# One GpSimd power of eight columns for two lengths in the block's residual sums

## The chip, the cores and the metric

The kernel runs on one core of a Trainium2 chip. The time is the device time of one execution in microseconds, as the median of several runs. The profile is one further execution, recorded by the hardware profiler; its times count from the first instruction of the span.

## What is computed

The reference is a stack of four stages over `x` (8 batches of 512 tokens, 256 features, float32): a mixture of experts, a segmented memory attention, a hyperbolic transformer block with adaptive layer norm, and two layers of windowed attention with a gated feed-forward. The change lies in the third stage, at its two residual sums:

```python
_norm = lambda x: sqrt(sum(x * x)).clip(EPS)          # EPS = 1e-7
logmap0 = lambda x: arctanh(clip(_norm(x), EPS, 1 - 1e-5)) * x / _norm(x)
expmap0 = lambda v: tanh(_norm(v)) * v / _norm(v)
def mobius_add(x, y):
    x2, y2, xy = sum(x * x), sum(y * y), sum(x * y)
    num = (1 + 2 * xy + y2) * x + (1 - x2) * y
    return num / (1 + 2 * xy + x2 * y2).clip(EPS)
...
attn_t = g_msa * logmap0(attn_out)
x = mobius_add(residual, expmap0(attn_t))
...
ff_t = g_mlp * logmap0(ff)
return mobius_add(residual, expmap0(ff_t))
```

Both sums take a projection `u`, which stands for a point of the ball by its tangent (`attn_out = expmap0(u)`). So `logmap0` of it is `u` times a factor `f` of at most 1 that holds its length under `MAX_LEN`, the arctanh of the clip. The tangent is then `gate * u * f`, its length `n`, and `y = tanh(n) / n` times it.

## The kernel before, in words

All 8 batches of 512 tokens lie in SBUF as `X`, tokens on the 128 partitions, in `NT` = 4 tiles of tokens a batch. A number per token is therefore a tile of 128 x 4. The instruction streams of the five engines are written out by hand: generators yield once a beat, and `Beats.advance` lets every live generator take one step a beat, the urgent ones first and the bulk ones last. What is issued earlier in this order stands earlier in the in-order queue of its engine.

`last_stages` runs the block. Its main loop has 32 steps a batch, in which `attention` issues scores (`s`), exponentials (`pt`, L1209) and values (`oT`). Beside it run, each as a generator: `block.begins` (layer norm and q, k, v of a later batch, with the evictions at L985 and sums at L975), `middle(b)` (squares of the heads' outputs, lengths, the scaling of `o` at L1250, one half on VectorE and one on GpSimd, its transposition `flip`, the output projection `wo`, and the first residual sum), and `end(b)` (layer norm, the scaling of `v` at L1289, the feed-forward with `f1` and `f2`, and the second residual sum). `end(b)` is started when a `middle` has finished and the step in the batch is `END_AT` = 4; in the last batch it is started as soon as a `middle` has finished. After the last attention step the drain follows: a loop (L1390 to L1399) in which the remaining `middle` and `end` run, and in every second beat one step of the windowed layers (`layers.beat`, up to `LAYERS_FIRST`). When nothing of the block is left, `until_end.close()` frees its memory, `open_rest` issues the layers' weight loads on the SP queue, and the layers go on with a step a beat. Their shifted rows `h<-X` (L1724, L1726) use the same SP queue.

A residual sum has two parts. `sums` takes the projection tile by tile: ScalarE squares `u` with an accumulated sum (`u2`, L1066), GpSimd multiplies by the gate (L1099), and VectorE forms the sums of (gate u)^2 (`a2`) and gate u x (`xa`) (L1069). `joined` makes the two factors per token from these and applies them: ScalarE scales `X` by `e` (L1147), VectorE adds `cb` times the gated tangent (L1142), in a loop of five beats.

Lengths come from `Norms`. `inverse` clamps a squared length at `EPS * EPS` (VectorE, L860), and raises it to the power -0.5: for at most `NT` columns by one GpSimd operation (L862), for wider ones by the eight VectorE operations of `rsqrt_steps` (L817 to L826). It yields a beat behind the power. `length` multiplies clamp and power to the length (L872). `shorten` turns the power into the factor f (L879).

`joined` now makes two such powers, one behind the other: `shorten(u2)` gives f; f squared times `a2` (L1119, L1120) is the squared length of the tangent, and `length` of that gives n and 1/n. Then ScalarE takes tanh(n) (L1122). The squared length of y is s * s * a2 (L1127, L1128). It yields a beat behind each power, one before the step of L1126, one before L1133 and one before the loop.

Of the kernel before, what the change touches and what calls it, by code (L numbers as in the profile page):

```python
# [14 lines left out]
ALU = mybir.AluOpType  # L15
# [5 lines left out]
NT = SEQ // P  # L21
# [35 lines left out]
EPS = 1e-7  # L57
MAX_TANH = float(np.float32(1.0 - 1e-5))

MAX_LEN = math.atanh(MAX_TANH)  # L60
# [749 lines left out]
def rsqrt_steps(nc, x, y, t):  # L810

    bits = lambda a: a.bitcast(mybir.dt.int32)
    mul, stt = nc.vector.tensor_mul, nc.vector.scalar_tensor_tensor
    nc.vector.tensor_scalar(bits(y), bits(x), -0.5, float(0x5F3759DF), ALU.mult, ALU.add)  # L817
    mul(t, x, y)
    mul(t, t, y)
    stt(t, t, -10.0 / 3, t, ALU.add, ALU.mult)  # L820
    yield
    stt(y, t, 5.0, y, ALU.add, ALU.mult)
    yield
    mul(t, x, y)
    stt(t, t, -27.0 / 1024, y, ALU.mult, ALU.mult)
    stt(y, t, 9.0 / 16, y, ALU.add, ALU.mult)  # L826
# [18 lines left out]
class Norms:  # L845
# [10 lines left out]
    def inverse(self, n2, tag):  # L856

        nc, w = self.k.nc, n2.shape[1]
        c, r = self.new(w, f"{tag}c"), self.new(w, f"{tag}r")
        nc.vector.tensor_scalar_max(c, n2, EPS * EPS)  # L860
        if w <= NT:
            nc.gpsimd.tensor_tensor(r, c, self.k.mhalf.to_broadcast([P, w]), ALU.pow)  # L862
            yield
        else:
            yield from rsqrt_steps(nc, c, r, self.new(w, f"{tag}t"))
        return c, r
# [149 lines left out]
def last_stages(k, A, out, block):  # L1016


    nc, tc = k.nc, k.tc
    D = DIM  # L1020
    nq = CH // 4
    bank, acc = block.bank, block.bank.acc
    bank.all = False
    S, Q, begun = block.S, block.Q, block.begun
    with ExitStack() as stack:
# [31 lines left out]
        def adaptive(b, lo, n, tag):  # L1057
            out = p.tile([P, n, D], F32, tag=tag, name=tag)
            nc.sync.dma_start(
                out=out.rearrange("p n d -> p (n d)"),  # L1060
                in_=k.ada[b : b + 1, lo * D : (lo + n) * D].to_broadcast([P, n * D]),
            )
            return out
# [9 lines left out]
        def flip(src, out):  # L1073

            for kc in range(2):
                tp = bank("flip")
                for t in range(NT):
                    k.tr(tp[:, t * P : (t + 1) * P], src[:, t, kc * P : (kc + 1) * P])
                yield URGENT
                nc.vector.tensor_copy(out[:, kc, :], tp)  # L1080
# [32 lines left out]
        def joined(nm, xs, x2, u, acc):  # L1113

            u2, a2, xa = acc
            mul, stt = nc.vector.tensor_mul, nc.vector.scalar_tensor_tensor
            f = yield from nm.shorten(u2)
            n3, s, e, cb = (nm.new(NT, f"j_{i}") for i in ("n3", "s", "e", "cb"))
            mul(n3, f, f)  # L1119
            mul(n3, n3, a2)  # L1120
            n, r = yield from nm.length(n3, "j_l")
            nc.scalar.activation(s, n, AF.Tanh)  # L1122
            mul(f, r, f)
            nc.vector.tensor_scalar(cb, x2, -1.0, 1.0, ALU.mult, ALU.add)
            yield
            mul(s, s, f)  # L1126
            mul(n3, s, s)  # L1127
            mul(n3, n3, a2)  # L1128
            stt(e, xa, 2.0, s, ALU.mult, ALU.mult)
            mul(cb, cb, s)  # L1130
            mul(s, x2, n3)
            yield
            stt(s, s, 1.0, e, ALU.add, ALU.add)  # L1133
            nc.vector.tensor_scalar_max(s, s, EPS)
            nc.vector.reciprocal(s, s)
            stt(e, e, 1.0, n3, ALU.add, ALU.add)
            mul(cb, cb, s)
            mul(e, e, s)
            yield
            for t in range(NT + 1):  # L1140
                if t:
                    nc.vector.scalar_tensor_tensor(  # L1142
                        xs[t - 1], u[:, t - 1, :], cb[:, t - 1 : t], xs[t - 1],
                        ALU.mult, ALU.add,
                    )
                if t < NT:
                    nc.scalar.activation(xs[t], xs[t], AF.Copy, scale=e[:, t : t + 1])  # L1147
                yield

        def tiles(b):  # L1150
            return [k.X[:, b * NT + t, :] for t in range(NT)]
# [68 lines left out]
        def middle(b):  # L1220

            middles.append(b)
            nm, o, x2, xs = norms["m"], S[b]["o"], S[b]["x2"], tiles(b)
            gate = adaptive(b, 2, 1, "ada_m")[:, 0, :]
            h2 = nm.new(NT * CH, "oh2")
            for t in range(NT + 1):
                if t:
                    nc.vector.reduce_sum(
                        h2[:, (t - 1) * CH : t * CH],
                        sq.rearrange("p (h d) -> p h d", d=CHD),  # L1230
                        AX.X,
                    )
                if t < NT:
                    sq = p.tile([P, D], F32, tag="sqm", name="sqm")
                    nc.scalar.activation(sq, o[:, t, :], AF.Square)
                yield
            w = yield from nm.shorten(h2, 1.0 / BETA_RATIO)
            nc.vector.tensor_mul(h2, h2, w)
            nc.vector.tensor_mul(h2, h2, w)
            o2 = nm.new(NT, "o2")  # L1240
            nc.vector.reduce_sum(o2, h2.rearrange("p (t h) -> p t h", h=CH), AX.X)
            f = yield from nm.shorten(o2)
            w3 = w.rearrange("p (t h) -> p t h", h=CH)
            nc.vector.tensor_mul(w3, w3, f.unsqueeze(2).to_broadcast([P, NT, CH]))
            for i in range(2):
                ts = slice(2 * i, 2 * i + 2)
                o3 = o[:, ts, :].rearrange("p t (h d) -> p (t h) d", d=CHD)
                w2c = w[:, 2 * i * CH : 2 * (i + 1) * CH]
                eng = nc.gpsimd if i else nc.vector
                eng.tensor_mul(o3, o3, w2c.unsqueeze(2).to_broadcast([P, 2 * CH, CHD]))  # L1250
            yield
            yield
            oT = k.area(3).rearrange("p (c n) -> p c n", c=2)
            yield from flip(o, oT)
            acc = [nm.new(NT, f"j_{i}") for i in ("u2", "a2", "xa")]
            pps = {}

            def project():
                for t in range(NT):
                    pps[t] = bank("wo")[:, :D]  # L1260
                    for kc in range(2):
                        k.mm(pps[t], oT[:, kc, t * P : (t + 1) * P], wo[:, kc, :], kc == 0, kc == 1)
                    yield

            def evict(t, out):
                nc.vector.tensor_add(out, pps[t], b_o)

            pr = project()
            next(pr)
            yield  # L1270
            for _ in sums(xs, o, gate, acc, evict, lambda t: t in pps):
                next(pr, None)
                yield
            if b == NB - 1:
                layers.open_wo()
            yield from joined(nm, xs, x2, o, acc)
            waiting.append(b)

        def end(b):

            nm, xs = norms[f"e{b % 2}"], tiles(b)
            rows = adaptive(b, 3, 2, "ada_e")
            v = p.tile([P, NT, D], F32, tag="v_e", name="v", bufs=2)
            v2, x2 = yield from modulated(
                nm, xs, rows[:, 0, :], rows[:, 1, :], v, block.junk[0]
            )
            f = yield from nm.shorten(v2)
# [5 lines left out]
            uT = p.tile([P, NFC, SEQ], F32, tag="uT", name="uT")  # L1293
            sq = p.tile([P, SEQ], F32, tag="sqs", name="sqs")
            pps, sqs, f2, made, summed = {}, {}, {}, [], []
            acc = [nm.new(NT, f"j_{i}") for i in ("u2", "a2", "xa")]

            def f1():
                for fc in range(NFC + 1):
# [51 lines left out]
            f = yield from nm.shorten(n2)  # L1351
# [6 lines left out]
            for _ in sums(xs, v, gate, acc, evict, lambda t: t in f2):  # L1358
                next(pr, None)
                yield  # L1360
            yield from joined(nm, xs, x2, v, acc)

        n = 8 * nq
# [4 lines left out]
        for i in range(8 - HEADS_AHEAD, NB * n + 2):  # L1370
            if i >= 0:
                next(steps, None)
            b, r = divmod(i + BEGIN_AHEAD, n)
            if r == 0 and b < NB:
                start(block.begins(b))
            if (i + HEADS_AHEAD) % 8 == 0 and 0 <= i + HEADS_AHEAD < NB * n:
                start(block.heads((i + HEADS_AHEAD) // 8))
            if waiting and (i % n == END_AT or i > (NB - 1) * n):
                start(end(waiting.pop(0)))
            beats.advance()  # L1380
            if len(begun) == NB:
                begun.clear()
                layers.open_weights()
# [5 lines left out]
        i, even = PROJECT_AT - 8 * TILES_AHEAD, True  # L1389
# [625 lines left out]
```

## Time and profile before

| what | us |
|---|---|
| median of 3 runs (3374.48 to 3377.88) | 3377.74 |
| the profiled execution | 3374.69 |
| its span, first to last instruction | 3372.9 |
| first and last start of L1122, the Tanh of joined | 1299.1 and 2047.0 |
| GpSimd's power in joined, L862 to `j_lr` (16, mean) | 1.084 |

The mean clock granted to TensorE is 0.974 of full speed. Reading: the page gives busy time by engine, and the span in 40 slices with the busy share in tenths. A row of a view by line names engine, operation, output <- input by the program's names, shapes and count. The chain of waits is the sequence of work that ended last, each piece released by the one before it. In a timeline, a row's own duration may overlap the next one's on its engine. VectorE's busy time in the stretch from 1890 to 1900 us is 8.69 us of 10, TensorE's 4.59, and from 1980 to 1990 us 7.04 and 3.82. The largest waits of TensorE in the span are

```profile
PE q L83 <- DVE hT L1529: 24.1, 10, 8.1
PE flip L87 <- DVE o L1250: 17.4, 8, 7.6
PE prT L87 <- POOL pr L1664: 12.0, 7, 3.9
PE s L83 <- ACT pt L1209: 7.3, 3, 3.5
PE flip L87 <- ACT v L1289: 6.9, 1, 6.9
```

with the total, the count and the longest of each in us.

### The profile page before, as it was taken

Reading aid. Unit: us, or ns where it says so; the run is one execution under the profiler, and the core shown is the slowest. Engines: PE = TensorE matmul, PEld = TensorE weight load, DVE = VectorE, ACT = ScalarE, POOL = GpSimd, SP = SyncE. Lnnn points to the kernel's source line nnn. Section 1 sums busy time; section 2 is a strip of 40 time slices with the busy share of each in tenths; the row PEclk is TensorE's granted clock in tenths of the full one; section 3 lists DMA queues with packets and bytes.
Section 4 is the critical chain, followed back from the end, with each engine's and each line's share of the span. In section 5 each row is a group of like instructions: output and inputs, shape, how many; then the busy total and the mean of one; then the engine's idle time right before and its main releaser. Section 6 shows DMA issues by size and latency. Waiting matters only on the chain.

```text
span 3372.9 us, 45689 instructions
## 1 busy us (share of the span) xinstructions
PE 3238.6 (96%) x16359; PEld 1875.6 (56%) x16359; DVE 1943.6 (58%) x6003; ACT 1714.9 (51%) x3626; POOL 968.2 (29%) x932
## 2 busy tenths in 40 slices
PE   9999999999999999999999777999999999999998
PEld 4444444456666643544444445666666666666665
DVE  3211111145657847778875667776666767777773
ACT  3112121244454477666666434666666666666663
POOL 2000000032322212333333333333333334433332
PEclk9999999999999999999999889999999999999999
DMA  5111111000000010000010001000000000000000
GB/s 195 59 42 53 56 59 58 0 9 14 8 17 19 21 46 11 10 6 10 10 35 7 12 2 64 4 4 4 4 4 5 4 21 25 17 18 17 17 16 28
DMA packets 37075, 85.30 MB, mean 25 GB/s; under 512 B 4931, under 2 KB 29504, under 8 KB 33776
## 3 DMA queue, kind: packets, MB, share of 16 engines
q0 software_dynamic: 5152, 42.52, 3.6%
q1 hardware_dynamic: 26960, 33.56, 3.1%
q10 hardware_dynamic: 4736, 6.29, 0.6%
q8 instruction: 130, 2.13, 0.3%
q14 instruction: 97, 0.79, 0.1%
HBM read 69.73 MB, written 8.44 MB: 23 GB/s over the span
## 4 chain that ended last, share of the span: by engine, by line
PE 62%; DVE 10%; ACT 4%; POOL 1%; issue 1%; DMA 0%; SPq 0%; ACTq 0%; POOLq 0%; DVEq 0%
PE f L83 6%; PE w L83 4%; PE o L83 4%; PE g L83 4%; PE wo L83 4%; PE a L83 4%; PE sc L83 3%; PE prT L87 3%; PE v L83 3%; PE s L83 3%; PE q L83 3%; PE k L83 3%; PE proj L83 3%; PE oT L83 3%; PE qkv L83 2%; PE qkTp L87 2%
## 5 line engine op out<-in xcount | busy, mean ns | idle before, releaser
L1664 POOL TENSOR_TENSOR pr<-pr,sums 128x1024 f32<-128x1024 f32 (+1 forms) x128 | 215.1, 1681 | 672.0 <-DVE sums L1663 650.4
L1652 ACT ACTIVATE pr<-pr,nmx,rn 128x256 f32<-128x256 f32 (+1 forms) x512 | 287.4, 563 | 177.4 <-DVE nmx L1637 177.0
L391 DVE TENSOR_TENSOR hT<-hT,wm 128x512 f32<-128x512 f32 x128 | 88.9, 695 | 474.8 <-ACT hT L387 364.3
L1209 ACT ACTIVATE pt<-s 128x512 f32<-128x512 f32 x512 | 264.3, 611 | 140.6 <-PE s L83 140.5
L387 ACT ACTIVATE hT<-ph,wR 128x512 f32<-128x512 f32 x128 | 87.9, 687 | 351.1 <-PE ph L83 351.1
L83 PE MATMUL ph<-ccT,wR 128*128 128x512 f32 x512 | 240.6, 592 | 0.0
L83 PE MATMUL py<-hT,wR 128*128 128x512 f32 x512 | 240.5, 592 | 0.0
L83 PE MATMUL s<-qkT,qkT 16*128 16x512 f32 x1024 | 185.3, 666 | 9.6 <-ACT pt L1209 7.3
L83 PE MATMUL w<-w2w,g 128*128 128x256 f32 x768 | 187.6, 383 | 0.0
L1630 DVE CUSTOM_DVE_ANT_0 pr<-sc,wB 128x256 f32<-128x256 f32 (+1 forms) x512 | 168.2, 383 | 0.3 <-PE sc L83 0.3
L83 PEld LDWEIGHTS w<-w2w,g 128*128 128x128 f32 x768 | 141.3, 190 | 46.2 <-issue 32.3
L87 PE MATMUL prT<-ident,pr 128*128 128x128 f32 x1152 | 154.2, 275 | 12.3 <-POOL pr L1664 12.0
L198 POOL DMA_INDIRECT wR<-in_w_e_dram,erow x16 | 15.7, 982 | 523.0 <-PE py L83 261.4
L83 PEld LDWEIGHTS py<-hT,wR 128*128 128x128 f32 x512 | 97.1, 190 | 123.2 <-issue 123.2
L83 PEld LDWEIGHTS ph<-ccT,wR 128*128 128x128 f32 x512 | 97.3, 190 | 122.5 <-issue 122.5
L83 PE MATMUL g<-hnT,w 128*128 128x512 f32 x320 | 153.6, 603 | 0.5 <-DVE hnT L1772 0.5
L87 PEld LDWEIGHTS prT<-ident,pr 128*128 128x128 f32 x1152 | 132.9, 143 | 37.3 <-POOL pr L1664 17.2
L83 PE MATMUL oT<-pt,v_aug 128*32 128x512 f32 x1024 | 146.1, 634 | 6.2 <-ACT oS L1174 4.7
L83 PE MATMUL a<-hnT,w 128*128 128x512 f32 x320 | 150.4, 592 | 0.0
L387 ACT ACTIVATE hT<-ph,wS 128x512 f32<-128x512 f32 x64 | 44.0, 687 | 175.3 <-PE ph L83 172.5
L83 PE MATMUL ph<-ccT,wS 128*128 128x512 f32 x256 | 124.2, 608 | 2.8 <-DMA wS<-in_w_s_dram 2.0
L1779 DVE SCALAR_TENSOR_TENSOR g<-a,cols,gl 128x512 f32<-128x512 f32 x80 | 59.9, 748 | 114.8 <-PE a L83 96.8
(410 smaller groups left out, 7201.0 us busy)
## 6 DMA issues: line engine op xcount, KB each, us to landing
x1d<-X SPq DMA_DIRECT2D x32, 128.0 KB
x<-x1d POOLq DMA_DIRECT2D x32, 128.0 KB, 2.4
h<-X SPq DMA_DIRECT2D x64, 63.5 KB
w<-in_w_d_dram SPq DMA_DIRECT2D x2, 1386.0 KB
X<-in_x_dram SPq DMA_DIRECT2D x4, 512.0 KB
wB<-in_w_b_dram SPq DMA_DIRECT2D x1, 2048.0 KB
ada_e<-ada SPq DMA_DIRECT2D x8, 256.0 KB
out_dram<-X ACTq DMA_DIRECT2D x16, 128.0 KB
```

The lines of the kernel that those rows point to most:

```text
L83: self.nc.tensor.matmul(out, lhsT=lhsT, rhs=rhs, start=start, stop=stop)
L87: self.nc.tensor.transpose(out, in_, self.ident[:n, :n])
L198: nc.gpsimd.indirect_dma_start(out=w, out_offset=None, in_=A["w_e"], in_offset=bass.IndirectOffsetOnAxis(ap=erow[:, b, j : j + 1], axis=0),)
L387: nc.scalar.activation(hT, ph, AF.Gelu_apprx_tanh, bias=w[:, 4 * HID + fc : 4 * HID + fc + 1])
L391: nc.vector.tensor_mul(hT, hT, wm[b][:, j, :])
L1209: nc.scalar.activation(pts[-1][:, h % 2, :], ss[h], AF.Exp, scale=1.0 / math.sqrt(CHD))
L1630: nc.vector.tensor_tensor_reduce(prs[-1][:, a, i % 2, :], s[:, a, :], win, 1.0, LEAST, ALU.add, ALU.max, nmx[:, pair, i % 2 : i % 2 + 1],)
L1652: nc.scalar.activation(pr[:, a, h, :], pr[:, a, h, :], AF.Exp, bias=nmx[:, 2 * half + a, h : h + 1], scale=rn[:, i : i + 1], accum_out=sum ...
L1664: nc.gpsimd.tensor_mul(prs[half], prs[half], s.unsqueeze(3).to_broadcast([P, 2, 2, nw * P]))
L1779: nc.vector.scalar_tensor_tensor(g[r, c, :], pa, cols(4 + c, r), gl[r], ALU.add, ALU.mult)
```

## The change

`u2` and `a2` become the two halves of one tile of eight columns, `nm.pairs`, and one clamp and one GpSimd power of eight columns give 1/|u| and 1/|gate u|. The limit of width up to which `inverse` uses GpSimd is raised to eight columns; no other caller has a width between five and eight. From the two: f = min(MAX_LEN / |u|, 1), n = a2 / |gate u| * f, clamped at EPS, and f / n by VectorE's reciprocal. y's squared length is tanh(n) squared. One of the yields goes with the second power, so all behind it in `joined` is issued a beat earlier than it was.

```diff
@@ Norms.inverse
         nc.vector.tensor_scalar_max(c, n2, EPS * EPS)
-        if w <= NT:
+        if w <= 2 * NT:
             nc.gpsimd.tensor_tensor(r, c, self.k.mhalf.to_broadcast([P, w]), ALU.pow)
             yield
@@ joined
             u2, a2, xa = acc
             mul, stt = nc.vector.tensor_mul, nc.vector.scalar_tensor_tensor
-            f = yield from nm.shorten(u2)
-            n3, s, e, cb = (nm.new(NT, f"j_{i}") for i in ("n3", "s", "e", "cb"))
-            mul(n3, f, f)
-            mul(n3, n3, a2)
-            n, r = yield from nm.length(n3, "j_l")
+            s, e, cb, f, n, y2 = (nm.new(NT, f"j_{i}") for i in ("s", "e", "cb", "f", "n", "y2"))
+
+            _, r = yield from nm.inverse(nm.pairs, "j_l")
+            nc.vector.tensor_scalar(f, r[:, :NT], MAX_LEN, 1.0, ALU.mult, ALU.min)
+            mul(n, a2, r[:, NT:])
+            mul(n, n, f)
+            nc.vector.tensor_scalar_max(n, n, EPS)
             nc.scalar.activation(s, n, AF.Tanh)
-            mul(f, r, f)
+            nc.vector.reciprocal(n, n)
+            mul(f, n, f)
             nc.vector.tensor_scalar(cb, x2, -1.0, 1.0, ALU.mult, ALU.add)
             yield
+            mul(y2, s, s)
             mul(s, s, f)
-            mul(n3, s, s)
-            mul(n3, n3, a2)
             stt(e, xa, 2.0, s, ALU.mult, ALU.mult)
             mul(cb, cb, s)
-            mul(s, x2, n3)
+            mul(s, x2, y2)
             yield
             stt(s, s, 1.0, e, ALU.add, ALU.add)
             nc.vector.tensor_scalar_max(s, s, EPS)
             nc.vector.reciprocal(s, s)
-            stt(e, e, 1.0, n3, ALU.add, ALU.add)
+            stt(e, e, 1.0, y2, ALU.add, ALU.add)
@@ middle and end, each
-            acc = [nm.new(NT, f"j_{i}") for i in ("u2", "a2", "xa")]
+            nm.pairs = nm.new(2 * NT, "j_ua")
+            acc = nm.pairs[:, :NT], nm.pairs[:, NT:], nm.new(NT, "j_xa")
```

## The prediction

> **What bounds the kernel now.** I read the page first, then the busy time by stretches, then the chain of waits inside two stretches, then single rows.
>
> ```profile
> PE 3238.6 (96%) x16359; PEld 1875.6 (56%) x16359; DVE 1943.6 (58%) x6003; ACT 1714.9 (51%) x3626; POOL 968.2 (29%) x932
> ...
> PE   9999999999999999999999777999999999999998
> ```
> TensorE is busy 96% of 3372.9 us; only three slices, some 1855 to 2110 us, fall to 7 tenths. The edited functions run only between 1290 and 2060 us. The view by stretches (window, length, then busy us of PE, PEld, DVE, ACT, POOL, and the clock) splits that:
>
> ```profile
> 1400.00:1500.00 100.00, 97.06 (x487) 49.06 (x486) 75.62 (x255) 65.31 (x147) 34.70 (x37) 0.93 0.04 9
> ...
> 1900.00:1950.00 50.00, 37.07 (x117) 21.15 (x116) 41.03 (x124) 18.35 (x46) 22.14 (x20) 0.84 0.05 16
> 1950.00:2000.00 50.00, 32.07 (x104) 19.38 (x103) 32.82 (x124) 17.99 (x54) 15.80 (x16) 0.70 0.01 3
> ```
> One batch of Block takes about 99 us (flips of `o` at 1343.4 and 1442.1) with TensorE at 97%. The drain, where the last batch has no attention left beside it, leaves TensorE 31 of 100 us idle and its clock down to 0.70. A change of this size can win something in two places: the drain, and any part of a batch where "busy" matmuls follow another engine. The chain of waits from 1410 to 1445 us shows such a part (start, length, what):
>
> ```profile
> 1438.54 0.02 issue
> 1438.56 0.18 DVE shc L860
> 1438.74 0.07 issue
> 1438.81 1.18 POOL shr L862
> 1439.99 0.02 issue
> 1440.02 0.18 DVE shr L879
> ...
> 1440.59 1.51 POOL o L1250
> 1442.10 0.04 issue
> 1442.14 1.54 PE flip L87 x6
> ```
> From 1416.3 to 1438.7 us every piece of it is VectorE; it ends in GpSimd's half of L1250, and TensorE's flips wait for that. The sums of `end` (joined) lie inside this VectorE run. The sums of `middle` do not: around 1473 to 1498 us the chain is TensorE nearly throughout.
>
> **VectorE's part.** Each of the 16 joined calls has 20 small VectorE operations now and 19 after (one fewer each). Their pieces on the chain of the batch above: 0.08 (L860) + 0.66 (L879, L1119, L1120, L860) + 0.24 (L872, L1123, L1124) + 0.79 (L1126 to L1131) + 0.75 (L1133 to L1138) = 2.52 us. A piece that reads its predecessor's output costs some 0.19 us with its issue gap, one that doesn't some 0.07. The new order: 0.08 + (0.09 + 0.07 + 0.19 + 0.19 + 0.20 + 0.19 + 0.08 = 1.01) + (0.08 + 0.07 + 0.19 + 0.07 + 0.09 = 0.50) + 0.75 = 2.34 us. That is 0.18 us less for each call that lies on the path; beside TensorE-bound work it is nothing.
>
> **What moves.** joined gives way once less, so all behind its first power is issued one beat (a round of the interleaved generators) earlier. In the order of the built program TensorE's own sequence is unchanged until the drain, because `end` starts at a fixed step of each 32. What does move in front of something: in five batches one `X<-v` update (L1142) now stands ahead of VectorE's half of L1250. In the chain above VectorE is just done with L975 when the power returns (1439.98 against 1439.99), so this update is fully exposed: 0.39 us (its increment on the chain at 1910.67 to 1913.8 is 0.40). ScalarE's Tanh moves too, in `middle`, ahead of four exponentials that it used to follow: it must wait for the fourth VectorE operation behind the power, some 0.85 us after ScalarE would have reached the exponentials (1477.45). The matmuls that read these start at 1483.70 and the last exponential ended at 1479.51, so 4.2 us cover it: nothing; without that cover it would be 7 x 0.85 = 6 us. No DMA is moved against another on its queue.
> Batches: 5 x (0.39 - 0.18) = +1.0 us.
>
> **The power of eight columns.** No row has one. The nearest is the same operation on four:
>
> ```profile
> L862 POOL TENSOR_TENSOR j_lr<-j_lc,mhalf x16: 1006/1012/1922, 1297.8 to 2045.4; 128x4 f32<-128x4 f32 x16
> ```
> (min/median/max in ns.) Low end: 1.01 us, if nothing depends on the width. High end without contention: GpSimd's multiplies of 256 and 512 columns take 753 and 1333 ns (L1099, L1317), so 173 ns are fixed, and 0.84 us of the power belongs to its four columns; doubled, 1.85 us. The Trainium skill (GPSIMD Engine Reference, section 3.1, Elementwise) gives some 2.6 cycles an element at 1.2 GHz for two inputs, an estimate of 9 ns for four more columns, so 1.02 us. But by that price the four-column power itself would be near the fixed cost and not six times it, so I take the row: 1.85 us. It replaces two powers of 1.01, of which only the first was ever waited for.
>
> Does the wider power hold VectorE up? The Trainium skill (SBUF — State Buffer, "SBUF: two separate sides") speaks against the change: VectorE and GpSimd take a shared pair of ports as an exclusive lock for a whole instruction, so that a VectorE operation with two SBUF inputs waits until GpSimd's ends. By it each power would block VectorE, for up to 1.85 us in place of 1.01, in the five exposed stretches some +4 us. The timeline says it for the adds of squares and not for the power (start, length):
>
> ```profile
> 1478.01 0.15 DVE L903 TENSOR_TENSOR log<-log,log 128x4 f32<-128x4 f32 x1
> ...
> 1478.42 0.16 DVE L905 TENSOR_TENSOR log<-log,log 128x4 f32<-128x4 f32 x1
> ...
> 1483.25 1.13 DVE L1127 TENSOR_TENSOR j_n<-j_s 128x4 f32<-128x4 f32 x1
> ```
> L905 runs at its usual 0.16 us within the power of 1478.18 to 1479.22; L1127 takes 1.13 us under an add of squares (1480.24 to 1485.71). So the port costs 0 here, with +4 us as the other end.
>
> Waits for its result: in the exposed stretch VectorE is busy with other work from 1423.87 (end of L860) to 1426.81 (L879), 2.9 us, so 1.85 us stay hidden. In the drain the cover is thinner.
>
> **The drain.** Counting the beats that the loops issue, it falls from 76 to 74, and ends at step 19 of the windowed layers, not 20: one such step (2.6 us each: 1313 us of the rest by some 500 steps) goes behind it. By its joined calls:
> - `end(5)`, 1888 to 1914 us: VectorE is the chain, but for the Ln table, the Tanh table and the Tanh on ScalarE (1896.4 to 1899.9), for which VectorE idles 0.73 us. The new order has that Tanh before the Ln table, where Exp's table serves. -0.73 - 0.18, and +0.5 because only 1.4 us of other VectorE work follow L860 before the result is read: -0.4.
> - `middle(7)`, 1932 to 1948: GpSimd loses a slot of 1.01 and one of 1.92 us and gets 1.85 ahead of the adds of squares; VectorE waits 0.47 us now, some 1.3 then. Its four-column operations swell to 0.8 to 1.2 us under the adds, in a pattern the order changes. I take 0, from -2 to +1.
> - `end(6)`, 1974 to 1994: only 0.55 us cover the power, +0.9 over today's 0.50 wait. TensorE waits 6.88 us for the flips of `v`, whose scaling (L1289) today stands behind a second set of exponentials on ScalarE (1988.98 to 1990.89); the new order puts it ahead: -1.9. Together -1.0.
> - `end(7)`, 2039 to 2078: the power is covered by 1.3 us (L1576), +0.4; -0.18. After it, L1731 waits 2.50 us for the shifted rows `h<-X`, which queue behind the layers' weights; the weights now get one step more of lead, so TensorE's 1.42 us behind that go. Together -1.2.
> Drain: -0.4 + 0 - 1.0 - 1.2 = -2.6 us.
>
> **Sum.** +1.0 - 2.6 = -1.6 us on the profiled execution: 3374.69 to 3373.1 (its span 3372.9, with 1.8 us around it). That execution lies 3.05 us under the median of the runs; on the median, 3377.74 - 1.6 = 3376.1 us. The range of this case alone is 3370 to 3383.
>
> **Rivals.**
> 1. The drain pays fully, and the power doesn't grow with its width. For it: 245 us by 76 beats is 3.2 us a beat; two fewer, less the step moved behind, is -3.8; the flips (-1.9) and the rows (-1.4) make it -7.1; a flat power takes off the added waits (0.5 + 0.8 + 0.9 + 0.4 = 2.6), +1.0 stays from the batches: -8.7, of which I leave some 1.5 for what is counted twice, since a shorter beat is partly the same flips. 3377.74 - 7.2 = 3370.5. Against it: the stretches are VectorE-bound, and VectorE keeps its work.
> 2. Slower: the eight-column power is slow where it meets VectorE's traffic. A row speaks for it: one four-column power took 1.92 us, which doubled is 3.8. It decides from 2.9 us, where the cover of the batches ends: 5 x 1.0 = +5 us there, and in the drain 4 x 1.95 = +7.8: 3376.1 + 12.8 = 3389. Against it: 1.92 is the largest of 16, the median 1.01.
> 3. It does nothing that can be measured because everything is hidden: 3377.7. This falls in the first case.
>
> **Chances.** About 0.2% (6.8 us) is what a measurement of this kernel can tell from no change. The sum above and the third rival: 0.67, within it. The first rival 0.18, faster. The second 0.15, slower. The range goes a little into both: 3369 to 3386.
>
> **What would show it.** Right: L862 with eight columns near 1.85 us, 16 GpSimd and 16 VectorE instructions fewer, flips of `o` 99 us apart, TensorE idle between 1880 and 2080 us less by 2 to 3 us. Wrong: the period of a batch moves by over 0.5 us; VectorE waits for L862 in a batch; ScalarE's exponentials appear as what TensorE waits for after 1475; the stall at the flips of `v` stays at 7 us. The weakest terms are the width's price, and the order in the drain, where a shift by one beat realigns every queue.

## The result, and the profile after

The changed kernel takes 3405.58 us in the median (3403.45 to 3408.84, 4 runs) against 3376.86 us before (3374.48 to 3377.88, 4 runs). The ratio is 1.0089, with a 95% interval of 1.0077 to 1.0101: slower by some 29 us. The profiled execution has a span of 3402.9 us, 30.0 more than before. The forecast was 3376.1 us, no change, with a range of 3369 to 3386.

The page of the changed kernel, its busy time:

```profile
PE 3255.0 (96%) x16359; PEld 1874.3 (55%) x16359; DVE 1945.4 (57%) x5987; ACT 1714.4 (50%) x3626; POOL 958.8 (28%) x916
```

VectorE and GpSimd have 16 instructions fewer each, as the change says; VectorE is busy for 1.8 us more all the same, GpSimd for 9.4 us less. TensorE, with the same 16359 matmuls, is busy for 16.4 us more. So part of the loss does not show as idle time: the rows of the same matmuls are longer, because they run at a lower rate or because a wait is hidden in them. The view by stretches, from the flips of `o` of the second batch to those of the sixth (window, length, then busy us of PE, PEld, DVE, ACT, POOL, and the clock), first before, then after:

```profile
1342.50:1738.00 395.50, 382.42 (x1920) 191.04 (x1920) 298.59 (x1005) 260.05 (x582) 136.74 (x145) 0.94 0.03 8
```
```profile
1341.60:1758.50 416.90, 395.18 (x1921) 188.09 (x1921) 297.77 (x998) 259.30 (x583) 131.68 (x137) 0.92 0.03 8
```

Four batches take 21.4 us more. TensorE's idle time in them grows from 13.1 to 21.7 us, and its busy time by 12.8 us for the same work. Each of them takes 102.3 to 105.9 us, where it took 98.8 to 99.0. The rest of the 30 us: 0.8 us are won before, 2.3 us in the next batch, 5.2 us are lost up to the last flips of `o` (1909.5 and 1932.9) and 6.6 us behind them. Over two thirds of the loss lie in the batches, where I had counted +1.0 us.

What TensorE waits for in those four batches (engine and line that waits, what it waits for, us in total, times, longest), before and after. The windows, 1340 to 1740 and 1340 to 1760, take in the flips of the second batch as well:

```profile
PE flip L87 <- DVE o L1250: 9.0, 5, 2.1
PE oT L83 <- ACT oS L1174: 2.6, 4, 0.7
PE flip L87 <- POOL o L1250: 1.4, 5, 0.5
PE s L83 <- DVE ccT L985: 1.1, 1, 1.1
```
```profile
PE s L83 <- DVE ccT L985: 8.2, 4, 2.0
PE s L83 <- DVE uT L1307: 6.5, 4, 1.6
PE oT L83 <- ACT oS L1176: 3.0, 4, 0.8
PE flip L87 <- ACT v L1292: 2.4, 3, 0.8
PE flip L87 <- DVE o L1252: 0.7, 1, 0.7
```

The wait that I had costed, for L1250 (L1252 now), is gone from the four batches: the 0.7 us left are those of the second batch's own flips. Two others have come: the scores `s` wait for VectorE's evictions `uT` (L1303 before, L1307 now) and `ccT` (L985). They don't read `uT`: the code's seven PSUM banks rotate among all users, and the last two of a group of eight `s` get a bank that this eviction has yet to empty. The timeline of VectorE ahead of that wait (start, length), before and after, and GpSimd's adds of squares beside it in the changed kernel:

```profile
1380.22 0.74 DVE L1303 TENSOR_SCALAR uT<-f,cols 128x512 f32<-128x512 f32 x1
...
1381.10 1.89 DVE L940 SCALAR_TENSOR_TENSOR ccT<-X,mv,wB 128x256 f32<-128x256 f32 x2
1382.91 0.74 DVE L1303 TENSOR_SCALAR uT<-f,cols 128x512 f32<-128x512 f32 x1
```

```profile
1379.67 0.74 DVE L1307 TENSOR_SCALAR uT<-f,cols 128x512 f32<-128x512 f32 x1
1380.33 0.15 DVE L1129 TENSOR_TENSOR j_y<-j_s 128x4 f32<-128x4 f32 x1
...
1380.98 1.14 DVE L1133 TENSOR_TENSOR j_s<-x,j_y 128x4 f32<-128x4 f32 x1
1382.04 1.88 DVE L940 SCALAR_TENSOR_TENSOR ccT<-X,mv,wB 128x256 f32<-128x256 f32 x2
1383.84 0.74 DVE L1307 TENSOR_SCALAR uT<-f,cols 128x512 f32<-128x512 f32 x1
```
```profile
1380.83 5.57 POOL L1321 TENSOR_TENSOR sqs<-sqs,sq 128x512 f32<-128x512 f32 x4
```

Between the last two `uT` there now stand the five small operations L1129 to L1133 of `middle`'s joined. They take 1.71 us together, since the fifth falls under GpSimd's adds of squares and takes 1.14 us. Before, three such operations stood there (L872, L1123, L1124) for 0.22 us, and the six operations that the five replace (L1126 to L1131) followed the `uT`, at 1384.19 to 1386.97. From one `uT` to the next it was 2.69 us and is 4.17. What TensorE does behind it, before and after:

```profile
1382.71 2.11 PE L83 MATMUL s<-qkT,qkT 16*128 16x512 f32 x8
1384.76 1.07 PE L83 MATMUL oT<-pt,v_aug 128*32 128x512 f32 x8
1385.76 3.72 PE L83 MATMUL f<-wC,uT 128*128 128x256 f32 x16
1389.40 1.14 PE L83 MATMUL s<-qkT,qkT 16*128 16x512 f32 x8
```
```profile
1381.88 1.13 PE L83 MATMUL s<-qkT,qkT 16*128 16x512 f32 x6
1384.63 1.88 PE L83 MATMUL s<-qkT,qkT 16*128 16x512 f32 x2 [1.62 <-DVE uT L1307]
1386.44 1.94 PE L83 MATMUL oT<-pt,v_aug 128*32 128x512 f32 x8
1388.31 5.38 PE L83 MATMUL f<-wC,uT 128*128 128x256 f32 x16
1393.61 1.14 PE L83 MATMUL s<-qkT,qkT 16*128 16x512 f32 x8
```

The changed kernel is 0.83 us ahead at 1381.9 and 4.21 us behind at 1393.6: 5.04 us are lost. From the start of `s` to that of `oT` it is 2.51 us more, of which 1.62 is the stall; the other 2.53 are matmuls at a lower rate: eight `oT` take 1.94 us and not 1.07, sixteen `f` 5.38 and not 3.72. The granted clock (third number from the end of the row) of 1384.6 to 1393.6 is 0.62; at the same place before it is 1.00. After, then before:

```profile
1384.60:1393.60 9.00, 8.96 (x26) 4.68 (x26) 5.70 (x15) 4.34 (x12) 2.99 (x3) 0.62 0.00 0
```
```profile
1383.76:1392.76 9.00, 9.00 (x55) 5.09 (x53) 7.24 (x22) 7.16 (x18) 4.39 (x4) 1.00 0.01 2
```

The place ahead of L985 is the same story: VectorE's timeline has the five operations again (`end`'s joined, 1435.10 to 1436.50), and one thing more:

```profile
1432.35 0.18 DVE L1125 RECIPROCAL j_n<-j_n 128x4 f32<-128x4 f32 x1 [0.70 <-ACT j_s L1124]
```
L1125 waits 0.70 us for ScalarE's Tanh. It writes its reciprocal over `n`, which the Tanh still reads. Over the kernel VectorE waits 6.9 us in 16 waits for that; the prediction has no such term.

### The profile page after: what moved, and what is told of

The parts are those of the page before. It is cut to its first block, busy times and chain, and to the rows that moved or that the text cites. A ratio compares the mean times of both kernels' runs of the same rounds, so it can differ in the third digit from the quotient of the medians.

```text
span 3402.9 us, 45648 instructions
## 1 busy us (share of the span) xinstructions
PE 3255.0 (96%) x16359; PEld 1874.3 (55%) x16359; DVE 1945.4 (57%) x5987; ACT 1714.4 (50%) x3626; POOL 958.8 (28%) x916
## 4 chain that ended last, share of the span: by engine, by line
PE 59%; DVE 12%; ACT 4%; issue 2%; POOL 2%; DMA 0%; ACTq 0%; POOLq 0%; DVEq 0%
PE f L83 5%; PE o L83 4%; PE w L83 4%; PE g L83 4%; PE a L83 4%; PE wo L83 4%; PE sc L83 3%; PE prT L87 3%; PE q L83 3%; PE v L83 3%; PE k L83 3%; PE proj L83 3%; PE s L83 3%; PE oT L83 2%; PE qkv L83 2%
## 5 line engine op out<-in xcount | busy, mean ns | idle before, releaser
L83 PE MATMUL oT<-pt,v_aug 128*32 128x512 f32 x1024 | 153.7, 665 | 6.2 <-ACT oS L1176 5.7
L83 PE MATMUL f<-wC,uT 128*128 128x256 f32 x512 | 126.6, 400 | 1.3 <-DVE uT L1307 1.3
```

The lines of the kernel that those rows point to most:

```text
L83: self.nc.tensor.matmul(out, lhsT=lhsT, rhs=rhs, start=start, stop=stop)
```

## The experiments

Theory of order: with a beat fewer, the five operations stand ahead of evictions that TensorE waits for. Rivals: the wide power, the wait for Tanh, the shorter drain, another PSUM bank for `s`, and, for the size of the loss, the slow matmuls. Ratios are to the kernel before, which had a median of 3374.31, 3375.76 and 3374.81 us beside experiments 1 to 4, 5 to 8 and 9 to 11.

**1. An empty beat behind the power, in both callers.**
```
 _, r = yield from nm.inverse(nm.pairs, "j_l")
+yield
```


> The changed kernel with one more empty beat behind the eight-column power in joined, so that everything behind it stands in the beat where it stood in the kernel before; power, arithmetic and instruction counts stay as changed. Order theory (five small operations of the sums, L1129 to L1133, and the wait for Tanh at L1125 now stand ahead of the evictions that TensorE waits for): the loss of some 29 us goes nearly all, 3375 to 3382 us, and TensorE no longer waits 1.6 us for uT near 1384. Power theory (the eight-column power, or its 1.63 us on GpSimd, holds VectorE up): the loss stays, 3400 or more.

3382.69 us, ratio 1.0021 (1.0014 to 1.0028), 0.7 us above the expected range. The wide power and the whole arithmetic are still there, and 23 of 30 us are gone, by the ratios; the wait for `uT` is gone too. The wide power is not the cause. But in this program the last two `s` of the group also have a bank that no `uT` empties (weight loads of `s` wait for `uT` in 4 places, 8 in the changed kernel), and so it is in experiments 2 and 11; what the order alone does is seen in 5 and 6. Four batches take 394.8 us (before 395.5); what is left lies behind: 83.9 us up to the last flips of `o` against 78.8.

**2. The empty beat in `middle` only.**
```
+if nm.name == "m":
+    yield
```


> The empty beat in the sums of middle only; the sums of end stay one beat early. Order theory: the stalls at uT (about +5.0 us a batch, between 1375 and 1396) go, those at the eviction of qkv before the flips of o (about +1.7 a batch) stay: some 4 x 5 = 20 of 29 us are won back, 3382 to 3388. If both places were one stall that only moves, 3400.

3378.81 us, ratio 1.0013 (1.0004 to 1.0022), better than expected; within the intervals it can't be told from the beat in both callers. Its waits in the four batches:

```profile
PE s L83 <- DVE ccT L985: 8.2, 4, 2.0
PE oT L83 <- ACT oS L1178: 3.0, 4, 0.8
PE flip L87 <- ACT v L1294: 1.7, 2, 0.8
```
The waits for `uT` are gone, those for L985 are as in the changed kernel, and yet four batches take 399.5 us. The wait ahead of the flips is thus worth some 4 us of its 8.2, for it takes the place of the old one at the flips.

**3. The empty beat in `end` only** (the same with `!= "m"`).

> The empty beat in the sums of end only; the sums of middle stay one beat early. Order theory: the stall at uT and what follows it stay, +5.0 us in each of four or five batches, while the place before the flips of o goes back: 3393 to 3400. If the sums of end were the cause (the stretch that the prediction took for the bound one): 3380.

3397.92 us, ratio 1.0065 (1.0048 to 1.0082). The waits of `s` for L985 shrink to 2.3 us in four, those for `uT` stay at 6.5 in four, and most of the loss with them. `end`'s sums, where I had looked for the risk, are the minor place.

**4. The reciprocal in another tile.**
```
-nc.vector.reciprocal(n, n)
-mul(f, n, f)
+nc.vector.reciprocal(y2, n)
+mul(f, y2, f)
```


> The changed kernel, its reciprocal written to another tile, so that VectorE need not wait until ScalarE's Tanh has read n (0.70 us at L1125 in the batch of 1432, 0.27 us near 1378). Order theory: the five operations still stand ahead of uT, so most of the loss stays; 0.7 us less ahead of the eviction of qkv: 3394 to 3403. If that wait is the cause of the stalls: 3380.

3398.17 us, ratio 1.0067 (1.0050 to 1.0084): some 7 us of the loss by the ratios (its interval and that of the changed kernel overlap, from 1.0077 to 1.0084), with the stall at `uT` down from 1.62 to 1.39 us. At most a contribution, not the cause.

**5. Only the five operations a beat later, in both callers; beats, power, Tanh and drain as changed.**
```
+yield
 mul(y2, s, s)
 ...
 mul(s, x2, y2)
-yield
 stt(s, s, 1.0, e, ALU.add, ALU.add)
```


> The changed kernel with the same number of beats, in which only the five operations L1129 to L1133 are issued one beat later, with the six that follow them; power, Tanh, the X updates and the fall of the drain by two beats stay as changed. Order theory: the five operations no longer stand ahead of uT, the stall of 1.62 us at s goes in each batch, and most of the 24 us that the empty beat in middle won come back by this alone: 3378 to 3388. Rival (the earlier Tanh, the earlier X updates or the shorter drain make the loss): it stays at 3400 to 3406.

3381.29 us, ratio 1.0016 (1.0008 to 1.0023). This is the narrowest of the repairs, and it wins 25 of 30 us. VectorE at the same place:

```profile
1379.21 0.74 DVE L1307 TENSOR_SCALAR uT<-f,cols 128x512 f32<-128x512 f32 x1
1379.87 0.87 DVE L940 SCALAR_TENSOR_TENSOR ccT<-X,mv,wB 128x256 f32<-128x256 f32 x2
1380.66 0.74 DVE L1307 TENSOR_SCALAR uT<-f,cols 128x512 f32<-128x512 f32 x1
```
The last `uT` follows 1.45 us behind the one before it. L940, which took 1.88 us under GpSimd's adds, now comes for the most part ahead of them (they start at 1380.37) and takes 0.87. Four batches take 395.5 us, as before the change. `s` has the same waits for VectorE in this built program as in the changed kernel (8 weight loads of it wait for `uT`, for 3.7 us and not 12.8), so it is the order and no other bank that removes the stall.

**6. The empty beat in `middle`, and the reciprocal in another tile** (2 and 4 together).

> The empty beat in the sums of middle only, together with the reciprocal written to another tile. Order theory: the two repairs add up where the wait for Tanh still stands ahead of an eviction (0.70 us before L985 in end): stall of 2.04 us at s before the flips of o shrinks, 3373 to 3377, the time of the kernel before or a little less. If the wait for Tanh only mattered together with the stall at uT: 3378 to 3380, as with the empty beat alone.

3386.35 us, ratio 1.0036 (1.0022 to 1.0049): a miss. Taking a wait away made it some 8 us slower than experiment 2, by the ratios, though 18 of 30 us are still won. VectorE's order is the same, but a score group has another bank in this built program, one that `uT` empties:

```profile
1381.78 1.13 PE L83 MATMUL s<-qkT,qkT 16*128 16x512 f32 x6
1383.42 1.12 PE L83 MATMUL s<-qkT,qkT 16*128 16x512 f32 x2 [0.51 <-DVE uT L1309]
1384.47 1.69 PE L83 MATMUL oT<-pt,v_aug 128*32 128x512 f32 x8
1386.09 4.74 PE L83 MATMUL f<-wC,uT 128*128 128x256 f32 x16
```
Even this stall of 0.51 us is followed by slow matmuls (4.74 us for sixteen `f`), in all four batches, which take 408.5 us (2: 399.5). That the bank alone makes the difference is read from the trace; no run isolates it.

**7. The empty beat in `middle` always and in `end` for the first six batches, and the reciprocal in another tile.**
```
-yield from joined(nm, xs, x2, v, acc)
+yield from joined(nm, xs, x2, v, acc, b < NB - 2)    # True in middle: an empty beat
```


> The empty beat in middle for all batches and in end for the first six, not for the last two, whose sums lie in the drain; reciprocal to another tile. With the empty beat everywhere the batches took 486.9 us from the second to the seventh flip of o (488.3 before) but the stretch after it 83.9 (78.8 before). If both readings hold and add up: 3370 to 3375, faster than before. If the loss after the seventh flip comes from the empty beat in middle: 3376 to 3382.

3386.44 us, ratio 1.0032 (1.0020 to 1.0043): a miss, with the same wait for `uT` as in 6 (2.0 us in four).

**8. Six memsets ahead of the last `uT`, on top of 6.**
```
+if i == NFC - 1:
+    for _ in range(6):
+        nc.vector.memset(idle, 0.0)
 nc.vector.tensor_scalar(uT[:, i, :], ...)
```


> The kernel with the empty beat in middle and no wait for Tanh, to which six memsets of 128 columns on VectorE are added ahead of the last uT eviction (L1307) in each of the eight end: extra work of about 0.5 to 1 us at the place where the changed kernel stalls. Theory that a stall costs more than itself (matmuls run at half rate for some 9 us after it): TensorE's wait at s grows by no more than the added work, but a batch grows by several times that, up to 5 us, 15 to 25 us in all. If the stall costs only itself: 8 x 1 = 8 us at most.

3395.60 us, ratio 1.0063 (1.0047 to 1.0078). The memsets take 1.46 us and the stall grows from 0.51 to 1.82 us, by 1.31; four batches take 415.2 us, 1.7 more each. So VectorE time put ahead of the last `uT` is lost nearly in full: it has next to no slack there. But it costs 1.3 times the added stall, not several times. From 2 to 6 a batch grows by 2.2 us with a stall of 0.51, but that figure understates the step: from the start of `s` to that of `oT` it is 1.26 us in 2 and 2.69 in 6, since the last two `s` then run alone. The expected multiple is not shown.

**9. TensorE kept busy through the stall of the changed kernel.**
```
-for kc in range(2):
+for kc in (0, 1) * (3 if fc == NFC - 1 else 1):
     k.mm(pp, w1[...], vT[:, kc, :], kc == 0, kc == 1)
```


> The changed kernel, in which TensorE issues the last pair of feed-forward matmuls (f, the eighth of eight) three times instead of once, into the same bank with the same result, so that it is busy for 2.0 us more just before it waits 1.62 us for uT. Its other waits stay as in the changed kernel. If the matmuls behind a stall run slow because TensorE stood still (the changed kernel lost 5.0 us there: 1.62 of waiting, 3.4 of slow matmuls), the added work fills the stall and wins 2 to 3 us in each of four batches or more, 3385 to 3400 against 3404. If a stall costs only itself: +0.4 us a batch and 2.0 elsewhere, 3405 to 3412.

3406.36 us, ratio 1.0093 (1.0076 to 1.0110). Locally it went as the theory of slow matmuls says:

```profile
1381.66 5.42 PE L83 MATMUL f<-vT,wC 128*128 128x512 f32 x12
...
1388.32 1.14 PE L83 MATMUL s<-qkT,qkT 16*128 16x512 f32 x8
1389.39 1.07 PE L83 MATMUL oT<-pt,v_aug 128*32 128x512 f32 x8
1390.39 3.72 PE L83 MATMUL f<-wC,uT 128*128 128x256 f32 x16
```
With four useless matmuls more (twelve records for four, 3.44 us and not the 2.0 expected), `oT` and `f` run at full rate, and the kernel, 3.01 us behind the changed one at 1379.6, is 0.43 us behind at 1394.0: 2.6 us won by adding work. Four batches take 411.9 us, 5.0 less. But the kernel with them loses 1.7 us in the period before, 7.0 in the fifth and 2.4 in the sixth, wins 4.0 behind the last flips, and the whole is not faster. The slow matmuls behind a stall are real, but filling it with this much is no repair.

**10. The same ahead of the flips of `o`, in the kernel before.**
```
+for _ in range(fill if kc == 0 else 0):    # fill is 4 for o, 0 for v
+    k.mm(tp, k.ident, wC[:, :SEQ])
 for t in range(NT):
     k.tr(tp[...], src[...])
```


> The kernel before the change, in which TensorE issues four matmuls of 512 columns (1.9 us at full rate) into the bank of the first flip of o, ahead of the flips, which overwrite them: it fills most of the 2.05 us for which TensorE waits for L1250 in each batch. If slow matmuls follow standing still (1441 to 1450 us, some 4 us lost a batch): 3358 to 3370. If the stall costs only itself, or VectorE's chain sets the pace anyway: 3374 to 3380.

3382.45 us, ratio 1.0023 (1.0015 to 1.0031): a miss. The clock in the four batches rises from 0.94 to 0.97, and the four batches take 394.8 us for 395.5. But the dose was twice what the expectation had reckoned: the four matmuls are eight records and take some 4 us, against a stall of 2.06.

```profile
1442.07 0.69 DVE L1252 TENSOR_TENSOR o<-o,shr 128x512 f32<-128x512 f32 x1
1442.18 1.50 POOL L1252 TENSOR_TENSOR o<-o,shr 128x512 f32<-128x512 f32 x1 [0.61 <-DVE shr L1246]
1442.52 4.09 PE L83 MATMUL flip<-wC,ident 128*128 128x512 f32 x8
1446.44 1.04 PE L87 MATMUL flip<-ident,o 128*128 128x128 f32 x8
```
Both halves of `o` are ready at 1443.68, and the flips start 2.76 us later, behind the useless matmuls. So this run says nothing against the slow matmuls, and what a fitting dose would do was not tried. Another 5.7 us are lost ahead of the four batches, at the first two flips, where the stall to fill is 0.64 and 1.22 us.

**11. As 7, with the reciprocal in place as in the changed kernel.**

> As the seventh experiment (empty beat in middle always, in end for the first six batches), but with the reciprocal in place as in the changed kernel. There s waits in no bank that a uT eviction frees late, as it did in the seventh. If that bank made the seventh slow: batches as with the empty beat everywhere (394.8 us for four), the stretch after the seventh flip as with it in middle only: 3369 to 3376. If not: 3380 to 3386.

3376.23 us, ratio 1.0002 (0.9994 to 1.0011). No wait of `s` for `uT` in the four batches, which take 394.0 us:

```profile
1342.80:1736.80 394.00, 387.64 (x1921) 187.64 (x1921) 294.31 (x997) 260.32 (x582) 132.76 (x137) 0.92 0.03 9
```
The granted clock is as low as in the changed kernel, 0.92, and costs no time that can be seen here: most of it falls behind the flips (0.53 from 1433 to 1451, where the kernel before has 0.72 from 1434 to 1452). As for the rest, the stretch from the seventh flips of `o` (1831.2) to the end takes 1542.1 us, against 1542.2 before. This is the changed arithmetic in the old order where the order matters (with the bank of experiment 1), and it takes the old time. No version here beats the kernel before.

## Why the prediction was wrong

**The step that failed** is "The sums of `middle` do not" (lie in a VectorE run) with "beside TensorE-bound work it is nothing". I read from a chain with TensorE in it that VectorE had slack there. It had none. In the very stretch that I had read, the chain of before shows the sign:

```profile
1476.37 1.07 PE s L83 x8
...
1481.66 2.04 PE s L83 x8
```
The second eight `s` take twice as long as the first; a batch earlier, at 1382.71, it is 2.11 us. The row shows no releaser, but the view of L1303 has `s`'s weight loads waiting for it 2.8 us in 4 waits: the last `uT` already ended last there. By the ratios of experiments 2 and 3, 26 or 22 of the 30 us belong to this place; experiment 5, which moves the five operations alone and at both places, wins 25. The sign that the prediction had named, a period of a batch that moves by over 0.5 us, came true.

**What moves** was counted one-sidedly. I looked for what now stands ahead of L1250 and found the X update (0.39 us). The same look at `uT` and L985 would have found five operations. The order of the built program had them.

**A missing term**: the reciprocal over `n` makes VectorE wait for ScalarE's Tanh (6.9 us in 16 waits). By experiment 4 it was worth some 7 us in the changed kernel, at the edge of what the runs resolve.

**A missing price**: waits were costed at their length. At 1384 us on the timeline, 2.53 of the 5.04 us lost are matmuls at a lower rate. The Trainium skill (TensorE: Matmul & The Clock Gate, "HAM oscillation — how this bites in real kernels") has as its abstract rule "no PE-idle gaps >~3.4µs"; by it the stalls of 1.62 and 0.51 us would have cost only themselves, and here they were followed by a granted clock of 0.62 and 0.81 over 9 us. The measurement decides: shorter stalls can count too. What share of the 21.4 us is this price stays open. The busy time grows by 12.8 us, but a busy row can hide a wait, as the 2.11 us do. And a low clock alone loses nothing: by (1 - clock) x length, an estimate from the views by stretches, the four batches give up 33 us in the changed kernel, 24 before, and 32 in experiment 11, which takes the time of before.

**The wide power** was mis-sized a little: 1.63 us where I took 1.85 between 1.01 and 1.85. The four added columns cost 0.62 us and not 0.84; the fixed part of 0.17 us had come from a multiply (L1099) and an add (L1317, taken for a multiply), not from a power. Its row:
```profile
L862 POOL TENSOR_TENSOR j_lr<-j_lc,mhalf x16: 1633/1634/1798, 1293.7 to 2069.5; 128x8 f32<-128x8 f32 x16
```
It stayed hidden in the batches, as said, and never took 3.8 us; in the drain VectorE waits 3.0 us for it in four waits. The rival that ended on the slower side had the right sign with the wrong mechanism.

**The lock on the ports** was judged rightly for the power and too lightly for the adds of squares: it cost 0 under the power, but the kind of row that the prediction shows under an add (L1127, 1.13 us) is just what came to stand in front of `uT` as L1133, with 1.14.

**The drain** was to win 2.6 us; from the seventh flips of `o` to the end it lost 11.9. TensorE's wait at the last flips of `v` did shrink, from 6.88 to 3.50 us, by more than the 1.9 predicted. But right behind it `f` waits 1.41 us for a copy (L1080) and the matmuls run slowly, so that the lag grows from 24.3 us (1991.75 and 2016.08) to 30.0 (1997.10 and 2027.14, the sixteen `f`) there. Which moved operation delays that copy was not tried. Experiment 11, with `middle` late and the two sums of `end` in the drain early, takes the time of before there: fewer beats in `end` there are neither a gain nor, in themselves, a loss.

**Right** were the counts, the power hidden in the batches, no wait of TensorE for the exponentials in the four batches, and that the arithmetic by itself is worth nothing that can be measured (experiment 11).

## What to carry to other kernels

A step that is issued earlier must be checked against every eviction that it now precedes on its engine, not only against the one that ends the known critical run. Where TensorE is 97% busy, a group that takes longer than its like, as eight `s` with 2.04 us for 1.07, can be a wait that already ends last; there is no slack there. An operation that writes over its input in place also waits for another engine's reading of that input, as L1125 did for the Tanh. Work that is added to fill a stall has to be measured first: here it ran twice as long as reckoned.

## What was not expected of the hardware

A stall of TensorE of 0.51 us was followed by sixteen `f` in 4.74 us for 3.72, one of 1.62 us by 5.38 us. Work added in front of the stall removed the slow stretch (experiment 9: 3.72 us). Not every short stall does this: one of 0.66 us at 1429.36 in the kernel before is followed by a granted clock of 0.59 up to 1433.5, one of 0.76 us at 1433.67 in the changed kernel by 1.00 up to 1439.4; what decides was not found. And a low clock need not cost time: the four batches take 416.9 us at 0.92 in the changed kernel, and 394.0 us at 0.92 in experiment 11. A GpSimd power costs 1.01 us for four columns and 1.63 for eight, so by an estimate from these two 0.16 us a column.
